# Four graph layers on one core: the last group's two graphs go separately, in turn, from the second MLP product on

## The chip, the cores and the metric

The kernel runs on one core of a Trainium2 chip. The metric is the device time of one execution in microseconds, the median of several; 2787.66 us before the change. The span in the profile (first to last instruction) is a little shorter, 2784.8 us.

## The reference

64 graphs of 256 nodes with 256 features each (float32), and one 256 x 256 adjacency matrix per graph. Four layers follow each other; each is `x = layernorm(x + layer(x, adj))`:

```python
# layer 0: attention, 4 heads of 64, masked by adj, output product, layer norm
# layer 1: attention, 8 heads of 32, on the normed rows themselves, then an MLP
x = x + out
y = layer_norm(x, gamma2, beta2)
mlp = gelu(y @ W1 + b1) @ W2 + b2            # W1 256 x 1024, W2 1024 x 256
return x + mlp
# layer 2: edge weights from two vectors per node
Wh = h @ W
e = leaky_relu(s1[:, :, None] + s2[:, None, :])   # s1 = Wh a1, s2 = Wh a2
h_prime = softmax(where(adj > 0, e, -big)) @ Wh
# layer 3: edge scores from the rows
s = einsum('bid,bjd->bij', hidden * a0, hidden)
out = softmax(where(adj == 1, leaky_relu(s), -big)) @ hidden
```

No graph ever needs another one.

## The kernel before, in words

Two graphs make a group (`G = 2`), so there are 32 groups. A group's rows lie as 4 blocks of 128 rows (`TB = 4`), 2 blocks for each graph (`QB = 2`); transposed rows lie as 128 features by 512 rows (`T = 512`). `usual_input` does all the work for ordinary inputs; checks gathered on the way end in a flag, and a second path is run when the flag says so (here it doesn't).

Each group is a Python generator, `group(g)`, that writes out a piece of its instructions and yields. The loop at the end of `usual_input` starts a new group every 15 steps (`PACE`) and asks each running group for its next piece in turn, so about three groups' instructions are mixed at any time. TensorE's instructions are tied to this written order by `in_order`; the framework orders those of the other engines. `REST` makes a group let some turns go at named places (for example `"xn": 1`, `"xT2": 1`, `"wh": 2`, `"e3": 2`). Once no group is left to start, fewer groups are mixed: first two, and in the end the last group alone.

The pieces from the second MLP product on, for all groups:
- `project` (L727, its add L746): `hT` by `W2`, 8 products per block, a row for the bias added as a product with `onesb`; the result plus `both` goes to `y`. With more than two chunks it yields after each block.
- `renormed` (L846): per graph `stats` (bn_stats L583, bn_aggr L584 on VectorE; variance plus epsilon L586 and its power L590 on GpSimd) and `scaled` (L598 on VectorE), which writes the normalised rows `xn`.
- `layer2` (L874): `transposed` (TensorE transposes L570 of all four blocks, copied by ScalarE at L614), `Wh` (copied at L885), exponentials of the small node vectors (L891), transposes of these, edge weights on VectorE (L898 per block, mask L899), then `values_of`.
- `layer3` (L904): transposes, a copy and a scaled copy by ScalarE (L909, L910), edge scores into one two-bank PSUM tile `ps`, two exponentials (L921, L922), their maximum and the mask on VectorE (L923, L924), then `values_of`.
- `values_of` (L859): the product of the edge weights with the values, per block, the reciprocal of the sum (L869), the scaled add of the residual (L870), and `renormed`.
- One output DMA per group (L953).

The tiles are allocated from pools by name: `act` has three buffers for each name (`AT_ONCE = 3`), so `xn`, `y`, `xT`, `v`, `qT`, `kT` and `z` are each reused by the third next tile of that name; `both` shares `xn`'s buffers. `ps_m` has four PSUM buffers (`pm`), `ps_s` has two (`ps`).

After the last group come the final checks (L974 to L986) and the branch on the flag (L995, L996).

Of the kernel before, what the change touches and what calls it, by code (L numbers as in the profile page):

```python
# [16 lines left out]
P = 128  # L17
N = 256
# [376 lines left out]
def usual_input(ctx: ExitStack, tc: tile.TileContext, a: dict, out: bass.AP, flag: bass.AP):  # L395
# [202 lines left out]
            nc.vector.tensor_scalar(dst[:, t, 0:D], src[:, t, 0:D], mv[:, q, 0:1], rstd[:, q:q + 1],  # L598
                                    ALU.subtract, ALU.mult)

    def to_psum(src, c):

        pt = ps_m.tile([P, T], F32, name="pm")
        for t in range(TB):
            transpose(pt[:, t * P:(t + 1) * P], src[:, t, c * P:(c + 1) * P], ident)
        return pt

    def transposed(src, scale=None, bias=None):

        dst = act.tile([P, NC, T], F32, name="xT")  # L610
        for c in range(NC):
            pt = to_psum(src, c)
            if scale is None:
                nc.scalar.copy(dst[:, c, :], pt)  # L614
            else:
                nc.scalar.activation(dst[:, c, :], pt, AF.Identity, bias=bias[:, c:c + 1], scale=scale[:, c:c + 1])  # L616
        return dst

    def scores(i, cs, qT, kT, mask, hd, scale, sums=None):
# [104 lines left out]
            go_on()  # L724
            yield

    def project(dst, srcT, w, extra, row=None):  # L727


        chunks = w.shape[1]  # L730
        for i in range(G):
            pm = ps_m.tile([P, QB, D], F32, name="pm")
            for q in range(QB):
                t = i * QB + q
                for c in range(chunks):
                    matmul(pm[:, q, :], srcT[:, c, t * P:(t + 1) * P], w[:, c, :],
                           start=c == 0, stop=c == chunks - 1 and row is None)
                if row is not None:
                    matmul(pm[:, q, :], onesb, row, start=False, stop=True)
                if chunks > NC:  # L740
                    yield
            o = dst[:, i * QB:(i + 1) * QB, :]
            if extra is None:
                nc.scalar.copy(o, pm)
            else:
                nc.vector.tensor_tensor(o, pm, extra[:, i * QB:(i + 1) * QB, 0:D], ALU.add)  # L746
# [61 lines left out]
    def layer1(xb, z, mask):  # L808

        zT = transposed(z, gamma1, beta1)  # L810
        x2 = act.tile([P, TB, D], F32, name="y")
        both = act.tile([P, TB, W], F32, name="both", tag="xn")
        yield

        def behind(i, oT, r):
            nc.vector.reciprocal(r, r)
            pt = ps_m.tile([P, QB, D], F32, name="pm")
            for q in range(QB):
                for c in range(NC):
                    transpose(pt[:, q, c * P:(c + 1) * P], oT[:, c, q * P:(q + 1) * P], ident)  # L820
            o = x2[:, i * QB:(i + 1) * QB, :]
            nc.vector.tensor_tensor(o.rearrange("p q (h d) -> p (q h) d", d=32), pt.rearrange("p q (h d) -> p (q h) d", d=32),
                                    r.rearrange("p q c h -> p (q c h)").unsqueeze(2).to_broadcast([P, QB * 8, 32]), ALU.mult)
            xi = xb[:, i * QB:(i + 1) * QB, :]
            nc.vector.tensor_tensor(o, o, xi, ALU.add)  # L825
            nc.gpsimd.tensor_tensor(both[:, i * QB:(i + 1) * QB, 0:D], o, xi, ALU.add)  # L826
            yield
            mv, rstd = stats(x2, i)
            scaled(xb, x2, i, mv, rstd[:, 0])
            yield  # L830

        yield from attention(zT, zT, z, mask, 32, gamma1, behind)
        yT = transposed(xb, gamma2, beta2)
        yield
        hT = act.tile([P, NF, T], F32, name="hT", bufs=1)
        for f in range(NF):
            pm = ps_m.tile([P, T], F32, name="pm")
            for c in range(NC):
                matmul(pm, w1[:, c, f * P:(f + 1) * P], yT[:, c, :], start=c == 0, stop=c == NC - 1)
            nc.scalar.activation(hT[:, f, :], pm, AF.Gelu, bias=b1[:, f:f + 1])  # L840
            if f % 2:
                yield
        yield from project(x2, hT, w2, both, b2m)
        return (yield from renormed(x2))

    def renormed(y, var=None):  # L846

        xn = act.tile([P, TB, W], F32, name="xn")
        nc.gpsimd.memset(xn[:, :, D:D + 1], 1.0)
        for i in range(G):  # L850
            mv, rstd = stats(y, i)
            if var is not None:
                nc.gpsimd.tensor_copy(var[:, i * QB:(i + 1) * QB], mv[:, :, 1])
            scaled(xn, y, i, mv, rstd[:, 0])
        yield
        yield from rest("xn")
        return xn

    def values_of(e, v, one, x, rs, var=None):  # L859

        y = act.tile([P, TB, D], F32, name="y")
        for t in range(TB):
            i, q = divmod(t, QB)
            po = ps_m.tile([P, one + 1], F32, name="pm")
            for kc in range(QB):
                matmul(po, e[:, i, kc, q * P:(q + 1) * P], v[:, i * QB + kc, 0:one + 1],
                       start=kc == 0, stop=kc == QB - 1)
            r = rs[:, t:t + 1]
            nc.vector.reciprocal(r, po[:, one:one + 1])  # L869
            nc.vector.scalar_tensor_tensor(y[:, t, :], po[:, 0:D], r, x[:, t, 0:D], ALU.mult, ALU.add)  # L870
        yield
        return (yield from renormed(y, var))

    def layer2(x, mask):  # L874
        xT = transposed(x)
        yield
        yield from rest("xT2")

        wh = act.tile([P, TB, W], F32, name="v")
        nc.gpsimd.memset(wh[:, :, D + 3:D + 4], 1.0)  # L880
        for tb in range(TB):
            pm = ps_m.tile([P, D + 3], F32, name="pm")
            for c in range(NC):
                matmul(pm, xT[:, c, tb * P:(tb + 1) * P], wx[:, c, :], start=c == 0, stop=c == NC - 1)
            nc.scalar.copy(wh[:, tb, 0:D + 3], pm)  # L885
        yield
        yield from rest("wh")


        ex = small.tile([P, TB, 3], F32, name="ex")  # L890
        nc.scalar.activation(ex, wh[:, :, D:D + 3], AF.Exp)  # L891
        pt = ps_m.tile([P, G, N], F32, name="pm")
        for t in range(TB):
            transpose(pt[:, t // QB, t % QB * P:(t % QB + 1) * P], ex[:, t, 0:1].to_broadcast([P, P]), ident)
        e = act.tile([P, G, QB, N], F32, name="qT")
        for t in range(TB):
            i, kc = divmod(t, QB)
            nc.vector.tensor_scalar(e[:, i, kc, :], pt[:, i, :], ex[:, t, 1:2], ex[:, t, 2:3], ALU.mult, ALU.max)  # L898
        nc.vector.tensor_tensor(e.rearrange("p g k q -> p (g k q)"), e.rearrange("p g k q -> p (g k q)"),  # L899
                                mask.rearrange("p g k -> p (g k)"), ALU.mult)  # L900
        yield
        return (yield from values_of(e, wh, D + 3, x, small.tile([P, TB], F32, name="r")))

    def layer3(g, x, mask):  # L904
        xT = act.tile([P, NC, T], F32, name="xT")
        xa = act.tile([P, NC, T], F32, name="z")
        for c in range(NC):
            pt = to_psum(x, c)
            nc.scalar.copy(xT[:, c, :], pt)  # L909
            nc.scalar.activation(xa[:, c, :], pt, AF.Identity, scale=a0[:, c:c + 1])  # L910
        yield
        ps = ps_s.tile([P, G, QB, N], F32, name="ps")
        for i in range(G):
            for kc in range(QB):
                for c in range(NC):
                    matmul(ps[:, i, kc, :], xT[:, c, i * N + kc * P:i * N + (kc + 1) * P],
                           xa[:, c, i * N:(i + 1) * N], start=c == 0, stop=c == NC - 1)

        e = act.tile([P, G, QB, N], F32, name="qT")
        low = act.tile([P, G, QB, N], F32, name="kT")  # L920
        nc.scalar.activation(e, ps, AF.Exp, bias=shift)  # L921
        nc.scalar.activation(low, ps, AF.Exp, bias=shift, scale=SLOPE)  # L922
        nc.vector.tensor_tensor(e, e, low, ALU.max)  # L923
        nc.vector.tensor_tensor(e.rearrange("p g k q -> p (g k q)"), e.rearrange("p g k q -> p (g k q)"),  # L924
                                mask.rearrange("p g k -> p (g k)"), ALU.mult)
        yield
        yield from rest("e3")
        return (yield from values_of(e, x, D, x, r_3[:, g], last[:, g]))

    def group(g):  # L930
        x, adj = load_group(g)
# [15 lines left out]
                                       accum_out=both_ways[:, g:g + 1])  # L947
        yield from rest("mask")
        xb, z = yield from layer0(g, x, mask)
        x = yield from layer1(xb, z, mask)  # L950
        x = yield from layer2(x, mask)
        x = yield from layer3(g, x, mask)
        nc.sync.dma_start(out[g * G:(g + 1) * G].rearrange("b (q p) d -> p (b q) d", p=P), x[:, :, 0:D])  # L953


    waiting = [group(g) for g in range(B // G)]
# [66 lines left out]
```

## Time and profile before

| What | Before |
|---|---|
| median of 3 runs, us | 2787.66 (2786.94 to 2789.51) |
| span in the profile, us | 2784.8 |
| instructions | 45617 |
| mean granted TensorE clock | 0.991 |
| ScalarE busy, us | 1295.8 (47%) |
| VectorE busy, us | 1931.9 (69%) |
| GpSimd busy, us | 578.4 (21%) |
| output DMAs | 32 of 512 KB, 2.9 us to landing (median) |

"Busy" is the time in which an engine runs an instruction. PE is TensorE's matrix products, PEld its weight loads, DVE VectorE, ACT ScalarE, POOL GpSimd. In a line of the timeline, `out<-in` are the tiles written and read, and `L598` is the line of the kernel. A float32 product stands as two records in the trace.

### The profile page before, as it was taken

What the parts mean: (1) busy time and instruction counts of PE and PEld (TensorE: products, weight loads), DVE (VectorE), ACT (ScalarE), POOL (GpSimd) and SP (SyncE); (2) the same over time, 40 slices, a digit from 0 to 9 for tenths busy, and PEclk for the clock granted to TensorE, in tenths of its full rate; (3) what the DMA queues carried; (4) which work ended last, traced back from release to release, by engine and by line L of the source; (5) the groups of instructions that cost most, each with busy time, mean ns of one, the idle gap of its engine ahead of it and who ended that gap; (6) DMA issues with size and microseconds to landing.
All of it is one profiled execution on the core that took longest, in us unless ns stands there. A gap on an engine that the chain in (4) does not pass through costs nothing.

```text
span 2784.8 us, 45617 instructions
## 1 busy us (share of the span) xinstructions
PE 2679.1 (96%) x17288; PEld 1842.6 (66%) x17288; DVE 1931.9 (69%) x6346; ACT 1295.8 (47%) x1953; POOL 578.4 (21%) x1138
## 2 busy tenths in 40 slices
PE   4899999999999999999999999999999999999996
PEld 2566666666667666667676667676666676666664
DVE  3666767776767776767776767777767777667764
ACT  2445445445444445444445444445444445444441
POOL 1112212212212212212212222212222212122211
PEclk9899999999999999999999999999999999999998
DMA  3000000000000000000000000000000000000000
GB/s 110 24 9 23 24 16 18 22 16 24 24 16 16 23 16 24 18 21 16 24 16 24 16 24 16 24 16 24 16 24 16 24 16 24 8 16 9 9 8 16
DMA packets 57905, 57.78 MB, mean 21 GB/s; under 512 B 5073, under 2 KB 57297, under 8 KB 57681
## 3 DMA queue, kind: packets, MB, share of 16 engines
q1 hardware_dynamic: 50784, 50.34, 5.9%
q10 hardware_dynamic: 6896, 4.47, 0.6%
q8 instruction: 139, 2.28, 0.3%
q14 instruction: 86, 0.70, 0.1%
HBM read 38.02 MB, written 16.78 MB: 20 GB/s over the span
## 4 chain that ended last, share of the span: by engine, by line
PE 68%; DVE 20%; POOL 8%; issue 2%; ACT 1%; DMA 1%; ACTq 0%; POOLq 0%; DVEq 0%
PE pm L567 53%; PE ps L567 9%; PE pm L570 6%; POOL rstd L590 6%; DVE xn L598 4%; DVE e L643 3%; DVE st L583 3%; POOL ve L586 2%; DVE z L598 1%; DVE mv L584 1%; DVE e L637 1%; ACT e L635 1%; DVE y L796 1%; DVE xb L802 1%; DVE xb L598 1%
## 5 line engine op out<-in xcount | busy, mean ns | idle before, releaser
L635 ACT ACTIVATE e<-ps 128x1024 f32<-128x1024 f32 x384 | 372.4, 1022 | 356.4 <-PE ps L567 353.3
L567 PE MATMUL pm<-L_gnn_W,hT 128*128 128x256 f32 x2048 | 463.2, 379 | 0.0
L567 PE MATMUL pm<-xT,L_gnn_W 128*128 128x512 f32 x1024 | 450.8, 593 | 0.0
L567 PEld LDWEIGHTS pm<-L_gnn_W,hT 128*128 128x128 f32 x2048 | 383.9, 190 | 63.2 <-issue 15.1
L643 DVE SCALAR_TENSOR_TENSOR e<-e,mask 128x256 f32<-128x256 f32 x1024 | 399.2, 453 | 29.2 <-ACT e L635 29.2
L840 ACT ACTIVATE hT<-pm,b 128x512 f32<-128x512 f32 x256 | 176.0, 688 | 477.8 <-PE pm L567 477.8
L586 POOL TENSOR_SCALAR ve<-mv 128x2 f32<-128x2 f32 x384 | 93.8, 244 | 1328.1 <-DVE mv L584 1131.9
L567 PEld LDWEIGHTS pm<-xT,L_gnn_W 128*128 128x128 f32 x1024 | 192.7, 191 | 216.6 <-issue 214.2
L590 POOL TENSOR_TENSOR rstd<-ve,mhalf 128x2 f32<-128x2 f32 (+1 forms) x384 | 298.4, 777 | 26.7
L583 DVE BATCH_NORM_STATS2 st<-y 128x6 f32<-128x256 f32 x768 | 299.8, 408 | 5.6
L598 DVE TENSOR_SCALAR xn<-y,mv,rstd 128x256 f32<-128x256 f32 x384 | 163.2, 471 | 127.6 <-POOL rstd L590 127.6
L923 DVE TENSOR_TENSOR qT<-qT,kT 128x1024 f32<-128x1024 f32 x32 | 39.2, 1225 | 195.2 <-ACT kT L922 195.2
L637 DVE TENSOR_TENSOR e<-e,mask 128x1024 f32<-128x1024 f32 x128 | 148.0, 1218 | 12.4 <-ACT e L635 12.4
L567 PE MATMUL pm<-e,z 128*32 128x256 f32 x2048 | 149.3, 385 | 3.5 <-DVE e L643 2.8
L567 PE MATMUL pm<-e,v 128*32 128x256 f32 x2048 | 135.5, 382 | 15.8 <-DVE e L637 15.8
L567 PE MATMUL ps<-xT 32*128 32x256 f32 x2048 | 148.0, 403 | 0.0
L826 POOL TENSOR_TENSOR both<-y,xb 128x512 f32<-128x512 f32 x64 | 81.7, 1276 | 313.2 <-DVE y L825 313.2
L764 POOL TENSOR_TENSOR x<-x,beta 128x1024 f32<-128x1024 f32 x32 | 75.7, 2365 | 324.7 <-PE pm L570 324.7
L616 ACT ACTIVATE xT<-pm,beta,gamma 128x512 f32<-128x512 f32 x128 | 92.9, 774 | 103.9 <-PE pm L570 103.6
L567 PE MATMUL ps<-qT,kT 64*128 64x256 f32 x1024 | 127.9, 389 | 0.6 <-ACT e L635 0.6
L567 PE MATMUL pm<-v,qT 128*128 128x260 f32 x512 | 120.3, 389 | 3.3 <-DVE qT L899 3.3
L567 PEld LDWEIGHTS ps<-xT 32*128 32x128 f32 x2048 | 93.3, 185 | 45.4 <-issue 42.1
(144 smaller groups left out, 4347.7 us busy)
## 6 DMA issues: line engine op xcount, KB each, us to landing
x<-in_x SPq DMA_DIRECT2D x32, 512.0 KB, 3.8
adj<-in_adj SPq DMA_DIRECT2D x32, 512.0 KB, 3.8
out<-xn SPq DMA_DIRECT2D x32, 512.0 KB, 2.9
L_gnn_W<-in_L_gnn_W ACTq DMA_DIRECT2D x2, 1024.0 KB, 7.3
L_gnn_WqT<-in_L_gnn_WqT ACTq DMA_DIRECT2D x1, 256.0 KB, 4.8
L_gnn_WkT<-in_L_gnn_WkT ACTq DMA_DIRECT2D x1, 256.0 KB, 6.7
L_gnn_WvT<-in_L_gnn_WvT ACTq DMA_DIRECT2D x1, 256.0 KB, 7.7
L_gnn_WoT<-in_L_gnn_WoT ACTq DMA_DIRECT2D x1, 256.0 KB, 8.9
```

Of the source, the lines that this page charges most:

```text
L567: in_order(nc.tensor.matmul(*args, **kw))
L570: in_order(nc.tensor.transpose(*args))
L583: nc.vector.bn_stats(st[:, q, :], src[:, t, 0:D])
L586: nc.gpsimd.tensor_scalar(ve[:, 0], mv[:, :, 1], EPS, None, ALU.add)
L590: nc.gpsimd.tensor_tensor(rstd, ve, mhalf[:, 0:k * QB].rearrange("p (k t) -> p k t", k=k), ALU.pow)
L598: nc.vector.tensor_scalar(dst[:, t, 0:D], src[:, t, 0:D], mv[:, q, 0:1], rstd[:, q:q + 1], ALU.subtract, ALU.mult)
L616: nc.scalar.activation(dst[:, c, :], pt, AF.Identity, bias=bias[:, c:c + 1], scale=scale[:, c:c + 1])
L635: nc.scalar.activation(e, ps, AF.Exp, scale=scale)
L637: nc.vector.tensor_tensor(e, e, mask.unsqueeze(1).to_broadcast([P, 2, QB * N]), ALU.mult)
L643: nc.vector.scalar_tensor_tensor(e[:, h, k], e[:, h, k], 1.0, mask[:, k], ALU.mult, ALU.mult, accum_out=sums[:, kc, c, j:j + 1])
L826: nc.gpsimd.tensor_tensor(both[:, i * QB:(i + 1) * QB, 0:D], o, xi, ALU.add)
L840: nc.scalar.activation(hT[:, f, :], pm, AF.Gelu, bias=b1[:, f:f + 1])
```

## The change

All functions from the second MLP product on take a list of graphs, `gs`, and work on its blocks alone. Groups 0 to 30 pass both graphs, as before. The last group makes two generators, one for each graph, and steps them in turn; the second begins two turns after the first (`parts[:turn // QB + 1]`). Each has its own tiles (`xn`, `y`, `xT`, `v`, `qT`, `kT`, `z`, `ps`), of which it fills its own half. It is meant to let one graph's work on one engine run beside the other's on another, in the stretch where no other group is left to fill the engines.

```diff
-    def to_psum(src, c):
+    def to_psum(src, c, gs=ALL):
...
-        for t in range(TB):
+        for t in blocks_of(gs):
             transpose(pt[:, t * P:(t + 1) * P], src[:, t, c * P:(c + 1) * P], ident)
...
-                nc.scalar.copy(dst[:, c, :], pt)
+                nc.scalar.copy(dst[:, c, on], pt[:, on])
...
-        nc.scalar.activation(ex, wh[:, :, D:D + 3], AF.Exp)
+        nc.scalar.activation(ex[:, at], wh[:, at, D:D + 3], AF.Exp)
...
-        nc.vector.tensor_tensor(e.rearrange("p g k q -> p (g k q)"), e.rearrange("p g k q -> p (g k q)"),
-                                mask.rearrange("p g k -> p (g k)"), ALU.mult)
+        eg = e[:, gs[0]:gs[-1] + 1].rearrange("p g k q -> p (g k q)")
+        nc.vector.tensor_tensor(eg, eg, mask[:, gs[0]:gs[-1] + 1].rearrange("p g k -> p (g k)"), ALU.mult)
...
-        nc.scalar.activation(e, ps, AF.Exp, bias=shift)
+        eg, low, ps = [t[:, gs[0]:gs[-1] + 1].rearrange("p g k q -> p (g k q)") for t in (e, low, ps)]
+        nc.scalar.activation(eg, ps, AF.Exp, bias=shift)
...
-        x = yield from layer1(xb, z, mask)
-        x = yield from layer2(x, mask)
-        x = yield from layer3(g, x, mask)
-        nc.sync.dma_start(out[g * G:(g + 1) * G].rearrange("b (q p) d -> p (b q) d", p=P), x[:, :, 0:D])
+        y, hT, both = yield from layer1(xb, z, mask)
+
+        def others(gs):
+
+            yield from project(y, hT, w2, both, b2m, gs)
+            x = yield from renormed(y, gs)
+            x = yield from layer2(x, mask, gs)
+            x = yield from layer3(g, x, mask, gs)
+            i, j = g * G + gs[0], g * G + gs[-1] + 1
+            nc.sync.dma_start(out[i:j].rearrange("b (q p) d -> p (b q) d", p=P), x[:, gs[0] * QB:(gs[-1] + 1) * QB, 0:D])
+
+        if g < B // G - 1:
+            yield from others(ALL)
+            return
+
+        parts = [others((i,)) for i in ALL]
+        turn = 0
+        while parts:
+            for r in parts[:turn // QB + 1]:
+                if next(r, END) == END:
+                    parts.remove(r)
+            turn += 1
+            yield
```

More of the change, by code (lines that the diff above doesn't have):

```diff
@@ L599, in scaled, with blocks_of, tokens, transposed @@
                                     ALU.subtract, ALU.mult)
-    def to_psum(src, c):
+    ALL = range(G)
+    def blocks_of(gs):
+        return range(gs[0] * QB, (gs[-1] + 1) * QB)
+    def tokens(gs):
+        return slice(gs[0] * N, (gs[-1] + 1) * N)
+    def to_psum(src, c, gs=ALL):
         pt = ps_m.tile([P, T], F32, name="pm")
-        for t in range(TB):
+        for t in blocks_of(gs):
             transpose(pt[:, t * P:(t + 1) * P], src[:, t, c * P:(c + 1) * P], ident)
         return pt
-    def transposed(src, scale=None, bias=None):
+    def transposed(src, scale=None, bias=None, gs=ALL):
+        on = tokens(gs)
         dst = act.tile([P, NC, T], F32, name="xT")
         for c in range(NC):
-            pt = to_psum(src, c)
+            pt = to_psum(src, c, gs)
             if scale is None:
-                nc.scalar.copy(dst[:, c, :], pt)
+                nc.scalar.copy(dst[:, c, on], pt[:, on])
             else:
-                nc.scalar.activation(dst[:, c, :], pt, AF.Identity, bias=bias[:, c:c + 1], scale=scale[:, c:c + 1])
+                nc.scalar.activation(dst[:, c, on], pt[:, on], AF.Identity, bias=bias[:, c:c + 1], scale=scale[:, c:c + 1])
         return dst
@@ L725, in attention, with project @@
             yield
-    def project(dst, srcT, w, extra, row=None):
+    def project(dst, srcT, w, extra, row=None, gs=ALL):
         chunks = w.shape[1]
-        for i in range(G):
+        for i in gs:
             pm = ps_m.tile([P, QB, D], F32, name="pm")
@@ L842, in layer1, with renormed @@
                 yield
-        yield from project(x2, hT, w2, both, b2m)
-        return (yield from renormed(x2))
-    def renormed(y, var=None):
+        return x2, hT, both
+    def renormed(y, gs, var=None):
         xn = act.tile([P, TB, W], F32, name="xn")
         nc.gpsimd.memset(xn[:, :, D:D + 1], 1.0)
-        for i in range(G):
+        for i in gs:
             mv, rstd = stats(y, i)
@@ L857, in renormed, with values_of @@
         return xn
-    def values_of(e, v, one, x, rs, var=None):
+    def values_of(e, v, one, x, rs, gs, var=None):
         y = act.tile([P, TB, D], F32, name="y")
-        for t in range(TB):
+        for t in blocks_of(gs):
             i, q = divmod(t, QB)
@@ L871, in values_of, with layer2 @@
         yield
-        return (yield from renormed(y, var))
-    def layer2(x, mask):
-        xT = transposed(x)
+        return (yield from renormed(y, gs, var))
+    def layer2(x, mask, gs):
+        xT = transposed(x, gs=gs)
         yield
@@ L880, in layer2 @@
         nc.gpsimd.memset(wh[:, :, D + 3:D + 4], 1.0)
-        for tb in range(TB):
+        for tb in blocks_of(gs):
             pm = ps_m.tile([P, D + 3], F32, name="pm")
@@ L890, in layer2, with layer3 @@
         ex = small.tile([P, TB, 3], F32, name="ex")
-        nc.scalar.activation(ex, wh[:, :, D:D + 3], AF.Exp)
+        at = slice(gs[0] * QB, (gs[-1] + 1) * QB)
+        nc.scalar.activation(ex[:, at], wh[:, at, D:D + 3], AF.Exp)
         pt = ps_m.tile([P, G, N], F32, name="pm")
-        for t in range(TB):
+        for t in blocks_of(gs):
             transpose(pt[:, t // QB, t % QB * P:(t % QB + 1) * P], ex[:, t, 0:1].to_broadcast([P, P]), ident)
         e = act.tile([P, G, QB, N], F32, name="qT")
-        for t in range(TB):
+        for t in blocks_of(gs):
             i, kc = divmod(t, QB)
             nc.vector.tensor_scalar(e[:, i, kc, :], pt[:, i, :], ex[:, t, 1:2], ex[:, t, 2:3], ALU.mult, ALU.max)
-        nc.vector.tensor_tensor(e.rearrange("p g k q -> p (g k q)"), e.rearrange("p g k q -> p (g k q)"),
-                                mask.rearrange("p g k -> p (g k)"), ALU.mult)
+        eg = e[:, gs[0]:gs[-1] + 1].rearrange("p g k q -> p (g k q)")
+        nc.vector.tensor_tensor(eg, eg, mask[:, gs[0]:gs[-1] + 1].rearrange("p g k -> p (g k)"), ALU.mult)
         yield
-        return (yield from values_of(e, wh, D + 3, x, small.tile([P, TB], F32, name="r")))
-    def layer3(g, x, mask):
+        return (yield from values_of(e, wh, D + 3, x, small.tile([P, TB], F32, name="r"), gs))
+    def layer3(g, x, mask, gs):
         xT = act.tile([P, NC, T], F32, name="xT")
         xa = act.tile([P, NC, T], F32, name="z")
+        on = tokens(gs)
         for c in range(NC):
-            pt = to_psum(x, c)
-            nc.scalar.copy(xT[:, c, :], pt)
-            nc.scalar.activation(xa[:, c, :], pt, AF.Identity, scale=a0[:, c:c + 1])
+            pt = to_psum(x, c, gs)
+            nc.scalar.copy(xT[:, c, on], pt[:, on])
+            nc.scalar.activation(xa[:, c, on], pt[:, on], AF.Identity, scale=a0[:, c:c + 1])
         yield
         ps = ps_s.tile([P, G, QB, N], F32, name="ps")
-        for i in range(G):
+        for i in gs:
             for kc in range(QB):
@@ L920, in layer3 @@
         low = act.tile([P, G, QB, N], F32, name="kT")
-        nc.scalar.activation(e, ps, AF.Exp, bias=shift)
+        eg, low, ps = [t[:, gs[0]:gs[-1] + 1].rearrange("p g k q -> p (g k q)") for t in (e, low, ps)]
+        nc.scalar.activation(eg, ps, AF.Exp, bias=shift)
         nc.scalar.activation(low, ps, AF.Exp, bias=shift, scale=SLOPE)
-        nc.vector.tensor_tensor(e, e, low, ALU.max)
-        nc.vector.tensor_tensor(e.rearrange("p g k q -> p (g k q)"), e.rearrange("p g k q -> p (g k q)"),
-                                mask.rearrange("p g k -> p (g k)"), ALU.mult)
+        nc.vector.tensor_tensor(eg, eg, low, ALU.max)
+        nc.vector.tensor_tensor(eg, eg, mask[:, gs[0]:gs[-1] + 1].rearrange("p g k -> p (g k)"), ALU.mult)
         yield
         yield from rest("e3")
-        return (yield from values_of(e, x, D, x, r_3[:, g], last[:, g]))
+        return (yield from values_of(e, x, D, x, r_3[:, g], gs, last[:, g]))
     def group(g):
```

## The prediction

> **What bounds the kernel now.** I read the page first, then the granted clock and engine busy time in short windows over the last 55 us, then the timeline and the chain that ended last in the same stretch.
>
> ```profile
> PE 2679.1 (96%) x17288; PEld 1842.6 (66%) x17288; DVE 1931.9 (69%) x6346; ACT 1295.8 (47%) x1953; POOL 578.4 (21%) x1138
> ...
> PEclk9899999999999999999999999999999999999998
> ```
>
> The reader is to see that TensorE is busy for 96% of the span at almost the full clock. Over the body only less TensorE work could help; the last of the 40 slices (70 us) is the exception, and there the change sits. The busy time by stage of the last group (columns: stretch, length, busy us and instructions on PE, PEld, DVE, ACT, POOL, granted clock, DMA):
>
> ```profile
> 2729.80:2733.30 3.50, 3.50 (x18) 3.03 (x17) 2.49 (x9) 0.00 (x0) 1.04 (x3) 1.00 0.00 0
> 2733.30:2739.70 6.40, 5.30 (x25) 3.67 (x23) 4.37 (x18) 2.79 (x7) 2.17 (x7) 1.00 0.00 0
> 2739.70:2743.70 4.00, 0.67 (x5) 0.43 (x5) 3.47 (x7) 0.00 (x0) 0.11 (x1) 0.84 0.37 131
> 2743.70:2751.20 7.50, 6.49 (x16) 4.87 (x16) 3.56 (x13) 0.00 (x0) 0.94 (x2) 0.63 0.00 0
> 2751.20:2756.30 5.10, 2.27 (x8) 1.38 (x8) 2.23 (x8) 1.17 (x3) 0.93 (x2) 0.64 0.00 0
> 2756.30:2761.80 5.50, 5.35 (x16) 3.82 (x16) 0.00 (x0) 1.12 (x4) 0.00 (x0) 0.71 0.00 0
> 2761.80:2766.50 4.70, 0.00 (x0) 0.00 (x0) 2.45 (x2) 2.07 (x2) 0.00 (x0) 0.98 0.00 0
> 2766.50:2771.90 5.40, 5.28 (x16) 4.07 (x16) 2.93 (x10) 0.00 (x0) 0.33 (x3) 0.70 0.00 0
> 2771.90:2784.80 12.90, 0.56 (x2) 0.50 (x2) 3.68 (x16) 0.00 (x0) 1.74 (x5) 0.68 0.14 47
> ```
>
> From 2733.3 on, the last group is alone and its stages stand in single file: transposes and Wh, edge weights on VectorE (TensorE idle), values, normalisation, transposes, scores, exponentials and mask (TensorE idle for 4.7 us), values, normalisation. The chain shows the hand-overs (start, length, what):
>
> ```profile
> 2740.47 1.91 DVE qT L898 x4
> 2742.41 1.24 DVE qT L899
> ...
> 2743.69 5.58 PE pm L567 x12
> ...
> 2756.36 5.37 PE ps L567 x16
> 2761.75 1.11 ACT qT L921
> 2762.87 1.01 ACT kT L922
> 2763.91 1.24 DVE qT L923
> 2765.16 1.24 DVE qT L924
> ```
>
> Each of these groups handles both graphs, though neither graph needs the other. The last normalisation writes start at 2775.99, the flag is ready at 2777.87, the span ends at 2784.8.
>
> [...] In windows of 1 us the clock is 1.00 or 0.50 but for single mixed ones (0.71 in 2742 to 2743, 0.88 in 2749 to 2750, 0.83, 0.76, 0.66, 0.64), which put the changes at 2742.4, 2749.2, 2752.7, 2759.5, 2766.3 and 2769.7[...]. [...] So 16 matmul records of values take 6.50 us here against 3.63 at 2729.83.
> [...] a VectorE product of 128x1024 takes 1.22 us, of 128x512 0.67 (L825); a ScalarE copy of 128x512 0.59, of 128x256 0.37 (L669).
>
> **The change part by part.** Up to the last group nothing moves: the built program has the same instructions in the same order on every engine. That also holds through the second MLP product of the last group and group 30's last values (PE order unchanged to 2733.46). I call the last group's graphs A and B.
>
> What is added in the tail: no matmul; ScalarE gets 9 more instructions (four copies, two scalings, two exponentials, one small one). Two halves cost over one whole about 0.1 to 0.2 us (copies 2 x 0.29 against 0.49 start to start; exponentials, taken from the 0.69 of a 128x512 activation, 2 x 0.56 against 1.01), in all 1.1 us, on an engine that is busy 7.15 of the last 44.6 us. VectorE gets three halved products (2 x 0.67 against 1.22, 0.1 each), GpSimd three memsets of 0.11. One output DMA becomes two; the last carries half, and the first lies under B's work.
>
> New waits, by the order in which tile slots are reused: A's layer-2 output takes the slot that group 30's output DMA reads. That DMA is issued at 2740.08 and lands 2.9 us later (4.8 at most in this trace), so by 2745 at the latest; behind the waiting memset on GpSimd stands A's variance, due at 2748.1. It costs nothing. B's first output takes the slot of `both`, free at 2730.7, before B needs it at 2733.3. B's Wh slot was freed by transposes at 2692.7, long before.
>
> What is moved I work out with the durations above, each engine in the built program's order[...]:
> - A's transposes run at 2733.3 to 2733.9 and no longer wait for B's normalised rows. A's Wh starts at 2734.55, when group 30's L870 frees a PSUM slot, and ends at 2736.5 (8 records of 0.239). B's transposes and Wh follow to 2739.2, A's exponent transposes to 2739.6.
> - A's edge weights are queued on VectorE behind group 30's normalisation, which ends at 2740.05: 2 x 0.475 + 0.67 give 2741.7. Before, the joint ones ended at 2743.63: 1.9 us won.
> - A's values: 2741.8 to 2744.6 (one block partly at full clock, one at half, 1.73). B's exponent transposes stand behind them, to 2745.4 with their tail; B's edge weights, mixed with A's rows on VectorE, end at 2747.9. B's values: 2748.0 to 2751.5 at half clock.
> - A's statistics, GpSimd's 1.0 us and A's normalised rows (to 2749.9) lie under B's values. A's transposes 2751.5 to 2752.6, ScalarE copies and scalings to 2753.7, A's scores to 2755.1 (full clock from 2752.7[...]). B's normalisation (rows ready at 2755.0) lies under A's scores.
> - ScalarE: A's exponentials 2755.3 to 2756.5, then B's copies to 2757.8. B's scores end at 2759.3. A's maximum and mask (to 2757.9) lie under that; A's values are behind B's scores on TensorE: to 2761.1.
> - B's exponentials to 2760.6 and its maximum and mask to 2762.6 lie in part under A's values; B's values 2762.65 to 2764.5. B's last statistics end at 2767.1 (A's rows stand between), GpSimd's 1.1 us, and the last rows start at 2768.3, against 2775.99.
>
> That is 7.7 us. The end after it (flag, branch, DMA landing: 8.8 us) stays. Running the same arithmetic over the old order gives 2774.7 to 2777.2[...], against 2775.99 measured, so its error is about a microsecond.
>
> The unknown is the clock[...]. [...] I take 2767.5: 8.5 us less.
>
> **The rivals.**
> (1) The clock never returns to full after 2742.4[...]. Then the last rows start at 2773.7: 2.3 us less, 2785.4, within 0.2%. [...]
> (2) The turns don't overlap: on in-order queues B's work stands in front of A's and the reverse, so the split costs its overhead (1.1 us on ScalarE) and one edge stage of one graph (1.6 us in layer 2, 1.3 in layer 3) more than now: +4.0, 2791.7, slower. For it: A's exponent transposes do stand behind B's Wh, and A's last values behind B's scores. Against: both were ready late anyway, and TensorE idles 18.7 of the 44.6 us from 2733.3 to 2777.9, which is room to overlap.
> (3) Full clock throughout[...]: last rows at 2764.9, 11.1 us less, 2776.6. For it: the gaps shrink from 3.3 and 4.8 us to some 2 to 3. [...]
>
> **How the numbers follow.** Forecast (a gain of 6.5 to 10 us): 0.68. Rival 3: 0.12. Rival 1: 0.15. Rival 2: 0.05. The time is 2787.66 - 8.5 = 2779.2. The range goes from rival 3 less the 1 us error (2775.5) to 2783.5[...]; that leaves out rival 2 and most of rival 1. 0.2% is 5.6 us: the forecast and rival 3 lie beyond it, rival 1 within it, rival 2 beyond it on the other side, which gives faster 0.80, same 0.15, slower 0.05.
>
> **What would show it.** Right: up to 2733.3 (or the same point counted from the end of the second MLP product) the two traces agree; A's values start about 2 us earlier than the joint ones; the TensorE gap ahead of layer 3's values shrinks from 4.8 to about 1.5 us; normalisation of A lies under TensorE work of B; mean clock between 2743 and 2770 above 0.7. Wrong: VectorE rows of one graph waiting long for a product of the other; a half clock up to the end; A's layer-2 rows waiting for the DMA of group 30; or a difference in the 2730 us before.

## The result and the profile after

The changed kernel takes 2776.64 us (median of 4 runs, 2775.21 to 2779.20), the kernel before beside it 2788.59 us: ratio 0.9959, 95% interval 0.9941 to 0.9976. Measured again on another occasion with three of the kernels below, it took 2777.48 us against 2786.33 us: ratio 0.9966, interval 0.9953 to 0.9979. So it gains 9 to 12 us; 8.5 were forecast (2779.2 us), and the measured 2776.64 us lies within the range given. One of the six executions of edges_first_filled, a kernel further below, took 6529.91 us and is left out of its figures; why it took so long is not known.

From the page of the profile after:

```profile
span 2777.4 us, 45647 instructions
...
PE 2677.1 (96%) x17288; PEld 1840.5 (66%) x17288; DVE 1932.8 (70%) x6349; ACT 1296.9 (47%) x1962; POOL 578.8 (21%) x1142
```

The same 17288 TensorE records, 9 more ScalarE, 3 more VectorE and 4 more GpSimd instructions.

The two profiles are set beside each other from the last group's first transposes on (2733.30 before, 2734.66 after; in eleven profiles of kernels that do the same work up to there, this point lies anywhere between 2731.21 and 2735.66, so the 1.36 us are not put down to the change). From there to the start of the last normalised rows it was 42.69 us before and is 34.83 us after: 7.86 us less. A second profile of the changed kernel (after_again below) has 34.78 us. The stages of after, in the columns used before:

```profile
2734.66:2741.05 6.39, 5.26 (x27) 3.99 (x25) 4.36 (x18) 2.67 (x9) 2.17 (x7) 1.00 0.00 0
2741.05:2743.18 2.13, 0.00 (x0) 0.03 (x1) 1.95 (x5) 0.34 (x2) 0.00 (x0) 1.00 0.39 133
2743.18:2747.10 3.92, 3.89 (x10) 2.72 (x10) 1.25 (x4) 0.00 (x0) 0.11 (x1) 0.56 0.18 61
2747.10:2749.71 2.61, 0.00 (x0) 0.03 (x1) 2.47 (x7) 0.00 (x0) 0.11 (x1) 1.00 0.00 0
2749.71:2756.83 7.12, 6.70 (x24) 4.75 (x24) 3.76 (x12) 1.79 (x5) 1.98 (x5) 0.76 0.00 0
2756.83:2758.39 1.56, 0.00 (x1) 0.00 (x1) 0.66 (x1) 1.56 (x5) 0.00 (x0) 1.00 0.00 0
2758.39:2762.35 3.96, 3.94 (x16) 2.87 (x16) 1.54 (x5) 1.85 (x4) 0.00 (x0) 1.00 0.00 0
2762.35:2763.92 1.57, 0.00 (x0) 0.03 (x1) 1.57 (x5) 0.00 (x0) 0.00 (x0) 1.00 0.00 0
2763.92:2769.49 5.57, 1.97 (x8) 1.41 (x8) 4.16 (x17) 0.00 (x0) 2.18 (x7) 1.00 0.14 49
2769.49:2777.40 7.91, 0.40 (x2) 0.34 (x2) 1.11 (x5) 0.00 (x0) 0.00 (x0) 0.58 0.13 40
```

The two long TensorE pauses of before (3.3 and 4.7 us) have become four of 2.13, 2.61, 1.56 and 1.57 us, and from 2754 to the last rows the granted clock stays at 1.00. The timeline of after shows where the halves lie beside each other in layer 3, and where they don't in layer 2 (start, length, engine, line, tiles, idle time before and what ended it):

```profile
2743.18 3.50 PE L567 MATMUL pm<-v,qT 128*128 128x260 f32 x8 [2.20 <-DVE qT L909]
...
2746.48 0.60 PE L570 MATMUL pm<-ident,ex 128*128 128x128 f32 x2
...
2747.19 0.54 DVE L907 TENSOR_SCALAR qT<-pm,ex 128x256 f32<-128x256 f32 x1 [0.30 <-PE pm L570]
...
2749.71 3.21 PE L567 MATMUL pm<-v,qT 128*128 128x260 f32 x8 [2.64 <-DVE mv L584]
...
2754.19 2.20 PE L567 MATMUL ps<-z,xT 128*128 128x256 f32 x8 [0.41 <-ACT z L920]
...
2755.47 0.73 DVE L598 TENSOR_SCALAR xn<-y,mv,rstd 128x256 f32<-128x256 f32 x2 [1.14 <-POOL rstd L590]
...
2757.73 0.69 DVE L934 TENSOR_TENSOR qT<-qT,kT 128x512 f32<-128x512 f32 x1 [1.52 <-ACT kT L933]
...
2758.39 2.20 PE L567 MATMUL ps<-z,xT 128*128 128x256 f32 x8 [1.56 <-ACT z L920]
...
2760.43 1.90 PE L567 MATMUL pm<-xn,qT 128*128 128x257 f32 x8
```

In layer 3 graph A's scores (2754.19) run while B is normalised (2755.47), A's maximum (2757.73) stands beside B's copies on ScalarE, A's mask beside B's scores (2758.39), and A's values follow without a pause. In layer 2 B's exponent transposes (2746.48) stand behind A's values on TensorE, so B's edge weights start only at 2747.19 and B's values at 2749.71. B's layer-2 rows are ready at 2756.20, 21.54 us after the first transposes; before, they were ready after 21.27 us. So B gains nothing in layer 2.

### The profile page after: what moved, and what is told of

Same layout as the page of the kernel before. It is cut to its first block, busy times and chain, and to the rows that moved or that the text cites. A ratio compares the mean times of both kernels' runs of the same rounds, so it can differ in the third digit from the quotient of the medians.

```text
span 2777.4 us, 45647 instructions
## 1 busy us (share of the span) xinstructions
PE 2677.1 (96%) x17288; PEld 1840.5 (66%) x17288; DVE 1932.8 (70%) x6349; ACT 1296.9 (47%) x1962; POOL 578.8 (21%) x1142
## 4 chain that ended last, share of the span: by engine, by line
PE 68%; DVE 20%; POOL 8%; issue 2%; ACT 1%; DMA 1%; ACTq 0%; POOLq 0%; DVEq 0%
PE pm L567 53%; PE ps L567 9%; PE pm L570 6%; POOL rstd L590 6%; DVE xn L598 4%; DVE e L652 3%; DVE st L583 3%; POOL ve L586 2%; DVE z L598 1%; DVE mv L584 1%; DVE e L646 1%; ACT e L644 1%; DVE y L805 1%; DVE xb L811 1%; DVE xb L598 1%
## 5 line engine op out<-in xcount | busy, mean ns | idle before, releaser
L567 PEld LDWEIGHTS pm<-L_gnn_W,hT 128*128 128x128 f32 x2048 | 383.9, 190 | 63.2 <-issue 15.1
L934 DVE TENSOR_TENSOR qT<-qT,kT 128x1024 f32<-128x1024 f32 (+1 forms) x33 | 39.3, 1192 | 187.3 <-ACT kT L933 187.3
L584 DVE BATCH_NORM_AGGREGATE mv<-st 128x2 f32<-128x6 f32 x768 | 121.5, 171 | 3.1
```

What stands on the lines that cost most here:

```text
L567: in_order(nc.tensor.matmul(*args, **kw))
L584: nc.vector.bn_aggr(mv[:, q, :], st[:, q, :])
```

## The experiments

All are compared with the kernel before on the same chip. "From first transposes to last rows" is the measure used above.

**Which layer's split brings the gain.** One kernel splits layer 3 alone, the other everything ahead of it (second MLP product to layer 2):

```diff
# layer3_only: both graphs together until layer 3
+        yield from project(y, hT, w2, both, b2m, ALL)
+        xl = yield from renormed(y, ALL)
+        xl = yield from layer2(xl, mask, ALL)
...
-            x = yield from layer3(g, x, mask, gs)
+            x = yield from layer3(g, xl, mask, gs)
# layer2_only: the two generators end with layer 2 and write one shared tile
+            x = yield from layer2(x, mask, gs, into)
...
+        yield from rest_of(into[0], ALL)      # layer 3 and the output, both graphs
```

> Both graphs together through layer 2, split in turn in layer 3 alone. In the two profiles graph B's layer-2 rows are ready 21.3 us (before: 2754.57 - 2733.30) and 21.5 us (after: 2756.20 - 2734.66) after the last group's first transposes, so theory 1 says that the whole gain is made in layer 3: the last rows start about 35 to 37 us after the first transposes (before 42.7, after 34.8), and the median is 5.5 to 8 us below before. Theory 2 (each split layer gives its share, about half): 39 us and 3 to 5 us below before. If the gain needs the whole overlap from the MLP on: under 2 us.

> Split from the second MLP product through layer 2, joined again for layer 3: the counterpart. Theory 1 (all of the gain is in layer 3): within 1.5 us of before, the last rows 41.5 to 43.5 us after the first transposes. Theory 2 (shares): 3 to 5 us below before.

layer3_only: 2779.44 us, ratio 0.9972 (0.9962 to 0.9982), 7.8 us below before's 2787.21. layer2_only: 2786.43 us, ratio 0.9997 (0.9988 to 1.0005). From the timelines, layer3_only (with A's scores) and then layer2_only:

```profile
2735.66 1.64 PE L570 MATMUL pm<-ident,xn 128*128 128x128 f32 x8
...
2755.39 3.50 PE L567 MATMUL ps<-z,xT 128*128 128x256 f32 x8 [0.62 <-ACT z L920]
...
2771.99 0.73 DVE L598 TENSOR_SCALAR xn<-y,mv,rstd 128x256 f32<-128x256 f32 x2 [0.40 <-POOL rstd L590]
```

```profile
2734.43 0.60 PE L570 MATMUL pm<-ident,xn 128*128 128x128 f32 x4
...
2777.00 0.73 DVE L598 TENSOR_SCALAR xn<-y,mv,rstd 128x256 f32<-128x256 f32 x2 [0.40 <-POOL rstd L590]
```

That is 36.33 and 42.57 us, against 42.69 before and 34.83 after. Theory 1 holds: splitting layer 3 alone gives 6.4 of the 7.9 us, splitting the rest alone gives 0.1. Most of the last 1.5 us is the clock: in layer3_only A's scores take 3.50 us, at half clock (0.50) up to 2758.5, and 2.20 in after, at full clock (1.00). A itself reaches its scores hardly earlier with both splits, 19.53 us after the first transposes against 19.73.

**Is it the overlap?** The second graph begins when the first is done:

```diff
-        parts = [others((i,)) for i in ALL]
...
+        for i in ALL:
+            yield from others((i,))
```

> The two graphs separate, but the second begins when the first is done, so nothing of one lies beside the other. If the gain is the overlap, graph B's MLP product (7.2 us) and its chain of some 31 us follow graph A's chain: 12 to 20 us slower than before. If the gain came from the smaller instructions or shorter pauses alone: no slower than before.

2805.38 us, ratio 1.0068 (1.0055 to 1.0082): 18 us slower than before. This edit also moves B's MLP product, 7.4 us long (2753.89 to 2761.34), behind A's chain; even if all of that is taken off, some 11 us are left. So the same small instructions without a neighbour lose; the overlap is what pays. The timeline shows B's product starting when A's last values are out:

```profile
2750.55 3.54 PE L567 MATMUL pm<-xn,qT 128*128 128x257 f32 x8 [2.90 <-DVE qT L935]
2753.89 3.77 PE L567 MATMUL pm<-L_gnn_W,hT 128*128 128x256 f32 x16
...
2794.29 0.73 DVE L598 TENSOR_SCALAR xn<-y,mv,rstd 128x256 f32<-128x256 f32 x2 [0.40 <-POOL rstd L590]
```

**What the half clock costs.** Spare products, never read, fill the pauses, in the kernel before and in the changed one:

```diff
+    def warm(n):
+        if n:
+            ps = ps_s.tile([P, G, QB, N], F32, name="ps")
+            for _ in range(n):
+                matmul(ps[:, 0, 0, :], woT[:, 0, 0:P], w1[:, 0, 0:N], start=True, stop=True)
# before_filled: warm(6) and warm(9) ahead of the values of layers 2 and 3,
#   warm(4) between the graphs' transposes of layer 3, last group only
# after_filled, in values_of:
+        if len(gs) == 1:
+            warm(4 if var is None else 2 * gs[0])
```

> The kernel before with spare products (weights by weights, never read) put in the last group's three TensorE pauses: 6 ahead of layer 2's values, 4 between the graphs' transposes of layer 3, 9 ahead of layer 3's values. The clock should stay at 1.00 to the end. If half clock costs the old tail what I worked out (last rows 37.5 us after the first transposes instead of 42.7), the median falls by 4 to 6 us. If the clock hardly matters for the chain: within 1.5 us.

> The changed kernel with spare products in its pauses: 4 ahead of each graph's layer-2 values, 2 ahead of graph B's layer-3 values. If the half clock still costs the split tail what I worked out (last rows 31.6 us after the first transposes at full clock, 34.8 in the profile of after): 2 to 4 us below after, some 13 us below before. If the overlap has already hidden it: within 1 us of after.

before_filled: 2782.16 us, ratio 0.9982 (0.9974 to 0.9989), 5.1 us below before. after_filled: 2774.97 us, ratio 0.9959 (0.9946 to 0.9972), 2.5 us below the changed kernel beside it (2777.48), though the two ratios' intervals overlap. Timeline of before_filled:

```profile
2740.47 2.76 PE L567 MATMUL ps<-L_gnn_W,L_gnn_WoT 128*128 128x256 f32 x12
2740.75 1.90 DVE L908 TENSOR_SCALAR qT<-pm,ex 128x256 f32<-128x256 f32 x4 [0.43 <-PE pm L570]
...
2743.97 3.77 PE L567 MATMUL pm<-v,qT 128*128 128x260 f32 x16 [0.73 <-DVE qT L909]
```

The spare products fill the wait for the edge weights, and the values behind them take 3.77 us at a granted clock of 1.00 instead of 6.50 at a mean of 0.57 in before. From first transposes to last rows: 37.38 us for before_filled (37.5 was the estimate), 31.70 for after_filled (estimate 31.6). In both the clock is at 1.00 up to the last products (from 2728 on in before_filled, from 2738 on in after_filled). So with the clock at 1.00 the split is worth 5.7 us; by difference, the other 2.2 of its 7.9 us are half clock that after does without: up to the last rows before has 0.50 for 17.1 us, after for 6.8.

**The wait in layer 2.** Graph B's edge weights are put ahead of A's values:

```diff
# edges_first, in layer2 ahead of values_of
+        if tuple(gs) == (0,):
+            yield
+            yield
# and at the start of layer3
+        if tuple(gs) == (1,):
+            yield
+            yield
```

> The changed kernel with two turns let go by graph A ahead of its layer-2 values and by graph B ahead of layer 3, so that graph B's exponent transposes and edge weights stand ahead of A's values and B's values follow A's at once. In after, B's edge weights wait for A's values on TensorE's queue, and B's values start 6.5 us after A's (2749.71 and 2743.18). If that wait is what keeps the layer-2 split from bringing anything, B's layer-2 rows are ready 2 to 3 us earlier (18.5 to 19.5 us after the first transposes, 21.5 in after) and the median falls by 1 to 3 us against after. If A's rows then merely wait on VectorE behind B's values: within 1 us of after.

> Both together: graph B's edge weights ahead of A's values, and spare products ahead of A's layer-2 values (4) and B's layer-3 values (2). If both causes are real and separate: 4 to 6 us below after, about 2771. If they overlap: no better than the better of the two.

> The changed kernel again, on the same chip as the three others, with more runs: about 2777, 10 to 12 us below before. Its single runs should spread by 3 to 4 us with the granted clock[...].

edges_first: 2775.26 us, ratio 0.9960 (0.9947 to 0.9973); edges_first_filled: ratio 0.9963 (0.9950 to 0.9976), median of five 2775.90 us; after_again: 2777.48 us, its runs from 2776.45 to 2778.12, a narrower spread than expected. Timeline of edges_first:

```profile
2731.21 0.60 PE L570 MATMUL pm<-ident,xn 128*128 128x128 f32 x4
...
2739.96 5.46 PE L567 MATMUL pm<-v,qT 128*128 128x260 f32 x16 [1.51 <-DVE qT L909]
...
2748.65 2.20 PE L567 MATMUL ps<-z,xT 128*128 128x256 f32 x8 [0.62 <-ACT z L926]
...
2749.18 0.74 DVE L598 TENSOR_SCALAR xn<-y,mv,rstd 128x256 f32<-128x256 f32 x2 [1.14 <-POOL rstd L590]
...
2763.94 0.73 DVE L598 TENSOR_SCALAR xn<-y,mv,rstd 128x256 f32<-128x256 f32 x2 [0.40 <-POOL rstd L590]
```

Both graphs' values now run as one block (x16), B's rows are ready 18.71 us after the first transposes (21.54 in after), the last rows start after 32.73 us (34.83). The profile is 2.1 us shorter; the medians lean the same way (2.2 us) without settling it.

What shortens it is not B's earlier rows but A's earlier scores. In after, A's layer-3 transposes stand behind B's values on TensorE, and A's scores start 19.53 us after the first transposes; in edges_first they start after 17.44. From there to the last rows it is 15.3 us in both, and in after_again and after_filled too. Nor are all of the 2.1 us the order's: with spare products in both and the clock at 1.00 up to the last products, the same order is worth 0.6 us (31.70 in after_filled against 31.06 in edges_first_filled2, below; their spare products don't all stand in the same places). The other 1.5 are, by difference, half clock that edges_first happens to avoid: up to its last rows it has 0.50 from 2740.2 to 2743.6 alone, after from 2743.5 to 2746.9 and from 2750.3 to 2753.8.

edges_first_filled missed its expectation: 32.44 us, 0.3 less than edges_first and 0.7 more than after_filled. Its timeline gives the reason: TensorE's pauses of 1.83 and 0.62 us had no filling, the clock fell at 2748.4 and stayed at 0.50 to 2751.8, and A's scores took 3.57 us instead of 2.20:

```profile
2747.16 0.78 PE L570 MATMUL pm<-ident,xn 128*128 128x128 f32 x4 [1.83 <-DVE xn L605]
2748.56 3.57 PE L567 MATMUL ps<-z,xT 128*128 128x256 f32 x8 [0.62 <-ACT z L935]
```

**Both together, all pauses filled, and the end.**

```diff
# edges_first_filled2: edges_first_filled, and in layer3
+        if tuple(gs) == (0,):
+            warm(4)
...
+        if tuple(gs) == (1,):
+            warm(2)
# before_two_outputs: the kernel before, last output DMA in two halves
+        for i, j in ((0, G),) if g < B // G - 1 else ((0, 1), (1, G)):
+            nc.sync.dma_start(out[g * G + i:g * G + j]...)
```

> Graph B's edge weights ahead of A's values, with spare products in all the pauses: 4 ahead of A's values, 4 ahead of A's layer-3 transposes, 2 ahead of B's scores, 2 ahead of B's layer-3 values. In edges_first_filled the clock still fell during A's scores (3.57 us instead of 2.20). If the two causes add, the last rows start 30 to 31 us after the first transposes (after_filled 31.70, edges_first 32.73) and the median is 1 to 2 us below after_filled, 2773 to 2774. If they are one and the same gain: within 1 us of after_filled.

> The kernel before with only the last group's output DMA divided by graph; nothing else moves. From the start of the last normalised rows to the end of the span it was 8.81 us in before and 7.91 in after (last DMA 512 KB, 2.9 us to landing, against 256 KB, 2.1 us). If the end waits for the landing, it falls to 7.9 to 8.1 here and the median by under 1 us. If the shorter end in after came from other things (the clock of the flag's product, chance): 8.5 to 8.9.

edges_first_filled2: 2773.69 us against 2788.00, ratio 0.9957 (0.9944 to 0.9971), the lowest median of all; from first transposes to last rows 31.06 us, 1.38 less than edges_first_filled, as much as A's scores gain by running at 1.00 (3.57 to 2.20 us, 1.37). It beats the kernel before; over the changed kernel its median is 3 to 4 us ahead, with overlapping intervals, and over after_filled the gain is not shown. before_two_outputs: ratio 1.0000 (0.9992 to 1.0008), and 8.09 us from the start of the last rows to the end of the span, against 8.81. The flag is ready equally late in both, 1.9 us after the last rows start, so the shorter end isn't the flag's doing.

## Why the prediction was right

It was right in direction and size, and in the mechanism. The time alone would not show that: the median (2776.64) lies at rival 3's number (2776.6), the execution that was profiled (2779.20) at the forecast's, and the body varies by more than the difference. The tail's own length decides: 34.83 and 34.78 us in the two profiles, where the schedule has 35.0 and rival 3 has 31.6. The profiles account for some 8.8 us (7.86 in the tail, 0.90 in the end), as much as the second comparison has; that these come so near to the 8.5 is in part luck, since the forecast had 8.5 in the tail and nothing in the end. The 12 of the first comparison are not accounted for beyond that; its interval reaches from 6.7 to 16.5 us. Two of its four executions (2775.34 and 2775.21 us) have a mean clock of 0.995 and 0.994 against 0.993 in the profiled one; whether their tails ran nearer to 1.00 isn't known, there is no trace of them. By its steps:

- Nothing moves before the last group's transposes: nothing in the profiles speaks against it; the 1.36 us shift is smaller than the spread of that point over all profiles (4.5 us). GpSimd has four more memsets, not three (the one of Wh's tile was not counted), at 0.11 us each.
- A's values start earlier: they start 8.52 us after the first transposes, the joint ones of before after 10.39; 1.9 us as worked out. What the prediction didn't say is that this advantage is gone one stage later. B's edge weights wait behind A's values, and B's rows come no earlier than before (21.54 against 21.27 us). Its own schedule had them at 2755.0, where the trace of before has 2754.57, and didn't draw the conclusion: layer 2's split alone is worth nothing, as layer2_only shows.
- The normalisation of one graph lies under products of the other, and the last pauses are 1.6 us each: yes, both seen at 2754.19 and 2758.39. The mean clock between 2743 and 2770 is 0.87 (0.69 before).
- The sum of 7.7 us, worked out with the clock at half from 2742.4 to 2752.7 and full from there on, as the author supposed: 7.86 measured. Not only the sum fits: counted from the first transposes, the schedule has B's layer-2 values at 14.7 us, the end of A's scores at 21.8, the end of B's at 26.0 and B's last values at 29.4; measured are 15.1, 21.7, 25.9 and 29.3. One detail differs. The schedule keeps the half clock through both graphs' layer-2 values; in after the clock fell to 0.50 at 2743.5, was at 1.00 from 2746.9 to 2750.3, where TensorE mostly waited (busy for 0.78 of 3.42 us), and at 0.50 again to 2753.8. In after_again it stayed at 0.50, as scheduled, from 2743.6 to 2753.8, and the sum was nearly the same (34.78 us to the last rows against 34.83). That the clock might change at other times, for which the forecast took another 0.8 us off (2767.5 instead of 2768.3), was the author's estimate; the two profiles don't show it.
- The wait for group 30's output DMA: the memset waited until 2744.45, A's variance came at 2749.75; nothing lost.
- "The end after it stays": this term was wrong. It took 7.91 us instead of 8.81. The last DMA carries 256 KB and lands after 2.1 us instead of 2.9, and the flag is ready 0.15 us earlier. The end was 8.2 to 8.8 us in three profiles whose last DMA has 512 KB (before, before_filled, layer2_only) and 7.3 to 8.1 in nine with 256 KB, before_two_outputs among them; the times of whole executions can't resolve it.

The output DMA lines of after show the two sizes (queue, count, size each, us to landing):

```profile
out<-xn SPq DMA_DIRECT2D x31, 512.0 KB, 2.9
out<-xn SPq DMA_DIRECT2D x2, 256.0 KB, 2.1
```

The rivals: a clock that stays half (1) didn't occur in the two profiles, where it was at 1.00 again from 2753.8 to the last rows; turns that don't overlap (2) didn't occur either, and its 4.0 us were not tested (one_after_other, 18 us slower, leaves out the overlap of whole chains); full clock throughout (3) didn't occur in the two profiles and is what after_filled brings about, whose 31.70 us stand against an estimate of 31.6.

## What to carry to other kernels

When several pieces of work are mixed to fill the engines, look at the stretch where the mixing runs out, and split what is left by independent parts. Find the stage in which the halves pass each other and put the split there: here layer 3 alone gave four fifths of it, and layer 2 by itself nothing. Then find the instruction from which the rest of the chain runs off unchanged (here A's scores) and see what stands ahead of it in its queue: in the profile it came earlier once the second half's vector work was put ahead of the first half's products. In this tail the clock was part of the chain: in before and after the products behind TensorE pauses of 2.1 to 4.8 us ran at a mean clock of 0.50 to 0.70, and of 2.1 us between two orders only 0.6 were left with the clock at 1.00.

## What the runs showed of the hardware

Read in stretches of 1 us from 2738 on, the granted clock in the tails is 1.00 or 0.50, with single stretches in between where it changes (0.71 in 2742 to 2743 of before, 0.75 in 2743 to 2744 of after). The same products take close to twice as long at 0.50: one graph's layer-2 values 3.80 us in after_again at 0.50, and 1.99 us in after_filled at 1.00.

Products behind a TensorE pause, with their mean granted clock:

| Kernel | Products | Pause before them, us | Their time, us | Granted clock |
|---|---|---|---|---|
| before | layer-2 values, both graphs | 3.32 | 6.50 | 0.57 |
| before | the last six layer-3 transposes | 2.10 | 1.65 | 0.50 |
| before | layer-3 values, both graphs | 4.82 | 5.28 | 0.70 |
| after | A's layer-2 values | 2.20 | 3.50 | 0.55 |
| after | B's layer-2 values | 2.64 | 3.21 | 0.60 |
| after | B's scores | 1.56 | 2.20 | 1.00 |
| after | B's layer-3 values | 1.60 | 1.97 | 1.00 |

The last pause alone doesn't tell. In edges_first and in edges_first_filled the same pauses of 1.83 and 0.62 us stand ahead of A's scores; in the first these took 2.20 us at 1.00, in the second 3.57 us, with 0.50 up to 2751.8. What decides when the clock changes was not shown by these runs.

In the seven profiles of kernels without spare products (all but one_after_other) the clock first fell to 0.50 between 8.9 and 9.5 us after the first transposes, though the time up to these varied by 4.5 us. Why is not known.
